# Attention scores from float16 pairs of q and k, one 128-row product a block, exponentials of 1536 columns

## The chip, the core and the metric

The kernel runs on one core of one Trainium2 chip. A core has five engines that run beside each other and wait for one another by semaphores: PE (matrix products into PSUM, eight banks of 512 float32 columns for each of 128 partitions), ACT (functions of one operand), DVE and POOL (arithmetic on tiles), and SP, which here only issues DMAs. The metric is the time of one execution on the device, in microseconds (us); lower is better.

## The reference, cut to what matters

Four layers follow each other on two images of 128 channels and 64 x 64 pixels. The change lies in the first, an attention over all 4096 pixels with four heads of 32 channels:

```python
xn = group_norm(x)                                  # 32 groups
q, k, v = split(w_qkv @ xn + b_qkv)                 # 128 channels each
q, k = rotary(q), rotary(k)                         # by row and column of the pixel
scale = 1 / sqrt(sqrt(32))
weight = einsum('bct,bcs->bts', q * scale, k * scale)       # per head, 4096 x 4096
weight = softmax(weight.astype(float16), axis=-1).astype(float32)
a = einsum('bts,bcs->bct', weight, v)
return xn + w_proj @ a + b_proj
```

The three others (a convolution layer with sampled positions, a 3x3 convolution layer, a state-space layer) are as before.

## The kernel before, in words

**Preparation** (`layer0`, to L253). The images are loaded and normalised into `xa`. For each of 16 blocks of 512 pixels (`rotated`, L177) PE makes two products each for q and k, DVE adds the bias and multiplies by the tables of cosines and sines (L184, L186), POOL adds the two (L188), SP stores the block to DRAM (`qd`, `kd`, L189), and DVE takes the largest magnitude a block later (L190). `values` (L193) makes v: two copies and a cast on ACT (L203, L205, L207), subtractions on POOL (L206, L208); v is kept as three bfloat16 parts and a column block of ones. After block 10 (`n == NBLK + 2`, L223) `load_head` brings the first head back from DRAM. From the largest magnitudes comes a flag (L235 to L250): where the product of the bounds on the norms of q and k is under 81 in each head, the exponentials need no subtraction of a maximum, and `attend` runs; else `attend_any`. This part's order on each engine is as written (`tc.manual_schedule`). The trace shows that `attend` ran.

**Attention** (`attend`, L268). For one head, q (32 channels x 4096 pixels, float32) is held four times, on partitions 0, 32, 64 and 96 of a tile `q4`; k lies in `k4`, each fourth block of 128 keys on another 32 partitions. The work is a list of 2048 units: image, head, block of 512 queries (`qb`, eight), block of 128 keys (`kb`, 32).

- `scores` (L283): one float32 product of 32 rows for each unit into a bank of `ps`; four units in a row lie on the four groups of 32 rows of the array. A group is two units (`GR = 2`), `ps` is a ring of three pairs of banks, and one ACTIVATE (L293) takes the exponential of 1024 columns into a float16 tile `e16` (eight of them).
- `weigh` (L298): for each unit one product of 128 rows, v (bfloat16, weights) by `e16`, added up in a bank `acc` (two) over the 32 key blocks (L303). Row 96 and on of `acc` are the sums of the exponentials.
- `normalise` (L309), after the 32nd: DVE takes the reciprocal (L314), copies it twice, multiplies the three parts (L320); POOL adds them into `att` (L321, L322).
- `project` (L326), for one query block after its last head: a float32 product of `att` by the projection's weights, into a tile of the ring `ps` (L329), added to `xa` by DVE (L331).

The loop (L337) issues four units' scores, then the weighted sums of four older ones; a projection is issued at `kb` 28 of the next query block. The loads of the next head (`load_head`, L259: four DMAs of q and four of k) are issued on SP in the current head. `k4` and `q4` have two tiles each, taken in turn. Outside the preparation the order on each engine comes from the Tile framework's scheduler, and rings of tiles give the waits.

Everything after L256 (the layers 1 to 3) starts when attention has ended.

Of the kernel before, what the change touches and what calls it, by code (L numbers as in the profile page):

```python
# [10 lines left out]
F32 = mybir.dt.float32  # L11
F16 = mybir.dt.float16
# [4 lines left out]
ALU = mybir.AluOpType  # L17
# [44 lines left out]
def img(t):  # L62
    return t.rearrange("p (r w) -> p r w", w=HW)
# [36 lines left out]
def layer0(g, I):  # L100
# [6 lines left out]
    with ExitStack() as ctx:  # L107
# [12 lines left out]
        k4 = [w.tile([P, L // BLK, P], F32, name=f"k4{i}") for i in range(2)]  # L120
# [5 lines left out]
        with ExitStack() as pctx:  # L126
# [119 lines left out]
            ok = pw.tile([1, NB, NH], F32, name="ok")  # L246
            nc.vector.tensor_scalar(ok, pr, 81.0, None, ALU.is_lt)
            okm = pw.tile([1, 1], F32, name="okm")
            nc.vector.tensor_reduce(okm, ok, AX.XY, ALU.min)
            nc.vector.tensor_copy(flag, okm)  # L250

        small = nc.values_load(flag[0:1, 0:1], min_val=0, max_val=1)
        with tc.If(small > 0) as cond:  # L253
            attend(g, v3, wpt, bo, qd, kd, q4, k4)
        with cond.Else():
            attend_any(g, v3, wp3, bo, qd, kd, q4)  # L256


def load_head(g, qd, kd, q4, k4, n):  # L259
    b, h = divmod(n, NH)  # L260
    rows = slice(h * CH, (h + 1) * CH)
    src = kd[b][rows, :].rearrange("p (j r m) -> p j r m", r=4, m=P)
    for r in range(4):
        g.nc.sync.dma_start(k4[n % 2][r * CH : (r + 1) * CH], src[:, :, r, :])
        g.nc.sync.dma_start(q4[n % 2][r * CH : (r + 1) * CH, :], qd[b][rows, :])


def attend(g, v3, wpt, bo, qd, kd, q4, k4):  # L268


    nc, tc = g.nc, g.tc
    NS = L // P
    GR = 2
    with ExitStack() as ctx:
        ap = ctx.enter_context(tc.tile_pool(name="l0ap", bufs=1))
        sm = ctx.enter_context(tc.tile_pool(name="l0asm", bufs=2))
        ep = ctx.enter_context(tc.tile_pool(name="l0ep", bufs=8))
        pss = ctx.enter_context(tc.tile_pool(name="l0pss", bufs=3, space=PSUM))
        psa = ctx.enter_context(tc.tile_pool(name="l0psa", bufs=2, space=PSUM))

        att = {}

        def scores(group):  # L283
            ps = pss.tile([P, GR, BLK], F32, name="ps")
            for i, (b, h, qb, kb) in enumerate(group):
                rows = slice((kb % 4) * CH, (kb % 4 + 1) * CH)
                nc.tensor.matmul(  # L287
                    ps[:, i, :], k4[h % 2][rows, kb // 4, :], q4[h % 2][rows, qb * BLK : (qb + 1) * BLK],
                    start=True, stop=True,
                )  # L290
            e = ep.tile([P, GR, BLK], F16, name="e16")
            n = len(group)
            nc.scalar.activation(e[:, :n, :], ps[:, :n, :], AF.Exp)  # L293
            return e

        acc = None

        def weigh(group, e):  # L298
            nonlocal acc
            for i, (b, h, qb, kb) in enumerate(group):  # L300
                if kb == 0:
                    acc = psa.tile([P, BLK], F32, name="acc")
                nc.tensor.matmul(acc, v3[b][:, kb, h, :], e[:, i, :], start=(kb == 0), stop=(kb == NS - 1))  # L303
                if kb == NS - 1:
                    normalise(b, h, qb, acc)
                    if h == NH - 1:
                        done.append((b, qb))

        def normalise(b, h, qb, acc):  # L309

            if qb == h == 0:
                att[b] = ap.tile([P, L], F32, name="att")
            rec = sm.tile([96, BLK], F32, name="rec")
            nc.vector.reciprocal(rec[0:32], acc[96:128])  # L314
            nc.vector.tensor_copy(rec[32:64], rec[0:32])
            nc.vector.tensor_copy(rec[64:96], rec[0:32])
            parts = sm.tile([CH, 3, BLK], F32, name="parts")
            for j in range(3):
                rows = slice(32 * j, 32 * j + 32)
                nc.vector.tensor_tensor(parts[:, j, :], acc[rows], rec[rows], ALU.mult)  # L320
            nc.gpsimd.tensor_add(parts[:, 0, :], parts[:, 0, :], parts[:, 1, :])  # L321
            nc.gpsimd.tensor_add(  # L322
                att[b][h * CH : (h + 1) * CH, qb * BLK : (qb + 1) * BLK], parts[:, 0, :], parts[:, 2, :]
            )

        def project(b, qb):  # L326

            pp = pss.tile([P, GR, BLK], F32, name="ps")
            nc.tensor.matmul(pp[:, 0, :], wpt, att[b][:, qb * BLK : (qb + 1) * BLK], start=True, stop=True)  # L329
            xv = interior(g, b, qb * RB, RB)  # L330
            nc.vector.scalar_tensor_tensor(xv, img(pp[:, 0, :]), bo, xv, ALU.add, ALU.add)  # L331
# [4 lines left out]
        held, done = [], []  # L336
        for u in range(0, len(units), 4):  # L337

            if done and u % NS == 4 * 7:
                project(*done.pop(0))  # L340

            for i in range(u, u + 4, GR):
                held.append((units[i : i + GR], scores(units[i : i + GR])))
            if len(held) > 8 // GR:
                for i in range(u, u + 4, GR):
                    weigh(*held.pop(0))

            b, h, qb, kb = units[u]
            if qb == 0 and kb == 12 and b * NH + h + 1 < NB * NH:
                load_head(g, qd, kd, q4, k4, b * NH + h + 1)  # L350
        for x in held:
            weigh(*x)
        for x in done:
            project(*x)


def attend_any(g, v3, wp3, bo, qd, kd, q4):
# [3 lines left out]
    with ExitStack() as ctx:  # L361
# [9 lines left out]
        for b in range(NB):  # L371
# [4 lines left out]
            def scores(qt, h):  # L376

                rows = slice(h * CH, (h + 1) * CH)
                s16 = at.tile([P, L], F16, name="s16")
                mx = sm.tile([P, 4], F32, name="mx")  # L380
                for j in range(4):
                    ps = pss.tile([P, 2, BLK], F32, name="ps")
                    for i in range(2):
                        k0 = (2 * j + i) * BLK
                        nc.tensor.matmul(
                            ps[:, i, :],
                            qr[rows, qt * P : (qt + 1) * P],
                            kr[rows, k0 : k0 + BLK],
                            start=True,
                            stop=True,  # L390
                        )
                    nc.vector.tensor_scalar(
                        s16[:, j * 2 * BLK : (j + 1) * 2 * BLK],
                        ps.rearrange("p a b -> p (a b)"),
                        1.0, None, ALU.mult, ALU.max, accum_out=mx[:, j : j + 1],
                    )
# [1432 lines left out]
def _constants():  # L1829
# [8 lines left out]
    scale = 1.0 / np.sqrt(np.sqrt(CH))  # L1838
# [98 lines left out]
```

## Time and profile before

| what | value |
|---|---|
| runs | 5787.97, 5789.0 (median), 5793.07 us |
| span of the profiled execution, first to last instruction | 5785.8 us |
| that execution's time with what lies around the span | not given apart; the median of the runs is 3.2 us above the span |
| granted PE clock over the span | 0.890 |
| preparation, to the first exponential | 121.1 us |
| attention, first exponential to the end of the last | 121.1 to 1247.5 us |
| last projection, to the first load of layer 1 | 1247.5 to 1259.9 us |
| layers 1 to 3 | 1259.9 to 5785.8 us |
| busy over the span: PE, DVE, ACT, POOL | 85%, 76%, 72%, 62% |

How to read it: the page of the profile gives busy times for the span, the same in 40 slices (about 145 us each; attention fills slices 2 to 8), the chain of work that ended last, and groups of instructions by line with the number of instructions, busy time, mean of one, and the idle time ahead of them with what ended it. An arrow `ps<-q,k` is the written tile and what is read. A float32 product stands in the trace as two matmuls, each with its own weight load; the trace gives a matmul's start, and its end is modelled, so that products in a row overlap. PEld is the loading of weights, PEclk the clock granted to PE, as a share of full speed.

### The profile page before, as it was taken

To read this page: it belongs to the slowest core of one execution; us is meant where nothing else is said; L and a number is where in the kernel's file an instruction comes from. 1 tells how busy PE (TensorE), PEld (TensorE's weight loads), DVE (VectorE), ACT (ScalarE), POOL (GpSimd) and SP (SyncE) were. 2 spreads that over 40 slices of the span, in tenths; PEclk is the share of its full clock that TensorE was granted. 3 is DMA by queue.
4 is the path that set the end of the run, shared out by engine and by line. 5 is a ranking of instruction groups with operands and counts; after the bars stand their busy time and mean duration, and the time that the engine had idled before them with its cause. 6 is when DMAs were issued, how large, how long until landed. Compare 5 with 4: busy or idle time off the path is not lost.

```text
span 5785.8 us, 58630 instructions
## 1 busy us (share of the span) xinstructions
PE 4889.5 (85%) x19110; PEld 1740.4 (30%) x19110; DVE 4400.7 (76%) x4135; ACT 4153.4 (72%) x6617; POOL 3602.9 (62%) x1139
## 2 busy tenths in 40 slices
PE   7999999989978789977877778777888877888776
PEld 3333333334434334422222222222222222222221
DVE  5333333355214599779999999999999999999998
ACT  4888888850025621289888888888888888888886
POOL 5111111110010031179999999999999999999998
PEclk8999999999989999988888888888877888877887
DMA  5000001030047400065555655556555555555564
GB/s 158 19 19 19 19 19 33 1 60 1 1 83 124 79 18 0 6 144 128 135 131 132 143 140 130 129 132 149 141 131 134 133 136 143 136 130 135 134 142 102
DMA packets 333114, 541.95 MB, mean 94 GB/s; under 512 B 66384, under 2 KB 121184, under 8 KB 331712
## 3 DMA queue, kind: packets, MB, share of 16 engines
q1 hardware_dynamic: 329664, 534.58, 39.7%
q10 hardware_dynamic: 3136, 3.56, 0.3%
q8 instruction: 151, 2.47, 0.2%
q14 instruction: 163, 1.34, 0.1%
HBM read 448.81 MB, written 89.13 MB: 93 GB/s over the span
## 4 chain that ended last, share of the span: by engine, by line
DVE 42%; PE 38%; ACT 10%; issue 5%; DMA 2%; POOL 2%; SPq 1%; DVEq 0%; POOLq 0%; ACTq 0%
DVE db L1524 28%; PE ps L287 11%; DVE db L1488 10%; PE acc L303 9%; PE m L1078 5%; PE m L566 5%; ACT da L1510 3%; PE acd L812 2%; ACT db L1516 1%; DVE gt L1551 1%; PE m L526 1%; ACT L1375 1%; ACT u L1375 1%; PE pf L775 1%; POOL db L1534 1%
## 5 line engine op out<-in xcount | busy, mean ns | idle before, releaser
L1534 POOL TENSOR_TENSOR db<-db,c 128x2048 f32<-128x2048 f32 x512 | 2313.2, 4533 | 45.4 <-ACT hl L1529 31.4
L1510 ACT ACTIVATE da<-dd,am 128x512 f32<-128x512 f32 x2048 | 1398.4, 687 | 299.1 <-DVE db L1524 280.1
L1524 DVE TENSOR_TENSOR_SCAN db<-da,db 128x512 f32<-128x512 f32 x1376 | 1585.0, 1203 | 34.6 <-ACT db L1516 26.6
L293 ACT ACTIVATE e<-ps 128x1024 f16<-128x1024 f32 x1024 | 992.2, 1021 | 134.2 <-PE ps L287 116.3
L1524 DVE TENSOR_TENSOR_SCAN db<-da,hl,db 128x512 f32<-128x512 f32 x672 | 825.9, 1271 | 40.3 <-POOL db L1497 3.0
L1488 DVE TENSOR_TENSOR db<-pbc,dd 128x2048 f32<-128x2048 f32 (+1 forms) x384 | 781.0, 2034 | 31.7 <-DMA dd<-dx 31.7
L1497 POOL TENSOR_TENSOR db<-b,dd 128x2048 f32<-128x2048 f32 (+1 forms) x192 | 773.2, 4027 | 13.0 <-DMA b<-bx 13.0
L1542 PE MATMUL py<-db,fold 128*32 128x512 f32 x4096 | 600.7, 672 | 151.8 <-POOL db L1534 151.8
L314 DVE RECIPROCAL rec<-acc 32x512 f32<-32x512 f32 x64 | 214.9, 3358 | 638.8 <-PE acc L303 612.1
L321 POOL TENSOR_TENSOR parts<-parts 32x512 f32<-32x512 f32 x64 | 80.4, 1256 | 974.8 <-DVE parts L320 974.8
L287 PE MATMUL ps<-q,k 32*128 32x512 f32 x4096 | 656.0, 642 | 3.6 <-DVE flag L250 2.8
L303 PE MATMUL acc<-e,v 128*128 128x512 f16 x2048 | 531.6, 382 | 0.0
L1516 ACT ACTIVATE db<-da,db,hl 128x1 f32<-128x1 f32 x1120 | 393.7, 352 | 147.3 <-DVE db L1488 103.8
L1078 PE MATMUL m<-v,u 128*128 128x512 f32 x864 | 380.0, 603 | 42.6 <-DVE v L1021 41.6
L1435 PE MATMUL pm<-dd,ident 128*128 128x512 f32 x512 | 357.5, 836 | 2.9 <-ACT dd L1428 2.7
L1467 PE MATMUL pbc<-bc,sel 64*128 64x512 f32 x384 | 208.7, 544 | 123.6 <-DVE db L1488 122.8
L303 PEld LDWEIGHTS <-v 128*128 128x128 bf16 x2048 | 158.3, 97 | 509.4 <-issue 388.0
L1394 PE MATMUL pm<-u,wxp 128*72 128x512 f32 x256 | 182.7, 855 | 141.4 <-ACT u L1375 141.4
L287 PEld LDWEIGHTS ps<-q,k 32*128 32x128 f32 x4096 | 229.7, 184 | 228.1 <-issue 145.2
L566 PE MATMUL m<-comb,w 64*128 64x512 f32 (+4 forms) x1296 | 269.9, 575 | 0.0
L686 POOL TENSOR_SCALAR yt<-y 32x512 f32<-32x512 f32 x8 | 18.2, 2271 | 381.3 <-DVE y L677 380.9
L1542 PEld LDWEIGHTS py<-db,fold 128*32 128x32 f32 x4096 | 89.8, 113 | 542.6 <-issue 313.0
(318 smaller groups left out, 6340.1 us busy)
## 6 DMA issues: line engine op xcount, KB each, us to landing
dd<-dx SPq DMA_DIRECT2D x1024, 256.0 KB, 6.5
dx<-dd SPq DMA_DIRECT2D x128, 512.0 KB, 5.5
c<-bx SPq DMA_DIRECT2D x1024, 64.0 KB, 2.1
hats<-pos SPq DMA_DIRECT2D x136, 256.0 KB, 9.7
b<-bx SPq DMA_DIRECT2D x512, 64.0 KB, 4.7
q<-qd SPq DMA_DIRECT2D x32, 512.0 KB, 7.4
w<-in_conv0T SPq DMA_DIRECT2D x18, 288.0 KB, 8.4
q<-in_x SPq DMA_DIRECT2D x8, 512.0 KB, 7.5
```

The costliest lines, as they stand in the source:

```text
L287: nc.tensor.matmul(ps[:, i, :], k4[h % 2][rows, kb // 4, :], q4[h % 2][rows, qb * BLK : (qb + 1) * BLK], start=True, stop=True,)
L293: nc.scalar.activation(e[:, :n, :], ps[:, :n, :], AF.Exp)
L303: nc.tensor.matmul(acc, v3[b][:, kb, h, :], e[:, i, :], start=(kb == 0), stop=(kb == NS - 1))
L566: yield lambda q=q, dy=dy, src=src, i0=i0, i1=i1: nc.tensor.matmul(m[:, i0 * NF : i1 * NF], w[half, dy, q, x, :], src, start=(dy == KC and ...
L1078: nc.tensor.matmul(m[x], weights[j][:, dy, x, :], v[j][b][:, x, r0 : r0 + RP, :].rearrange("p r i -> p (r i)"), start=(dy == 0), stop=(dy ...
L1488: nc.vector.tensor_tensor(db_tile(k)[:, :, :n], G[k].pop("pb")[:, :n].unsqueeze(1).to_broadcast([P, 4, n]), S[i]["d4", hf][:, 1, :, :n], A ...
L1497: nc.gpsimd.tensor_tensor(db_tile(k)[:, :, n:], S[i]["b", ng][:, n:].unsqueeze(1).to_broadcast([P, 4, BLK - n]), S[i]["d4", hf][:, 1, :, n ...
L1510: nc.scalar.activation(da, S[i]["d4", hf][:, 0, q, :], AF.Exp, scale=am[:, hf, q, ng : ng + 1])
L1516: nc.scalar.activation(b0, da[:, first : first + 1], AF.Identity, bias=b0, scale=hl[:, hf, ng, q, :])
L1524: nc.vector.tensor_tensor_scan(d1, d0, d1, 0.0 if zero else hl[:, hf, ng, q, :], ALU.mult, ALU.add)
L1534: nc.gpsimd.tensor_mul(v, v, S[i]["c", ng].unsqueeze(1).to_broadcast([P, 4, BLK]))
L1542: nc.tensor.matmul(S[i]["y", hf][32 * q : 32 * q + 32, :], fold, G[k]["db"][:, q, :], start=False, stop=(ng == NNG - 1),)
```

## The change

`k4` goes. Each of the two `q4` tiles (16 KB a partition) is seen as a float16 tile `qk` of two halves: q at `[:, 0]`, k at `[:, 1]`, both for 4096 pixels. q and k are scaled up by `UP = 64` in the tables of cosines and sines; the scores are scaled down by 64 squared in the exponential. A value t becomes a pair: its rounding to float16 and the remainder t - rounded, also in float16. Over the four groups of 32 partitions q holds rounded, remainder, rounded, remainder and k holds rounded, rounded, remainder, remainder, so that one product of 128 rows adds all four cross terms.

The rounding is a copy of 128 x 1024 (`split`: ACT for the first head, POOL later), the remainder a subtraction on DVE (64 partitions for k, twice 32 for q). The float32 data comes in pieces of 1024 columns on all four groups (`fetch`: four DMAs), through two staging tiles; the first head's k comes whole into the second `q4` tile. During a head the pieces of the next are fetched at `kb` 4 of query blocks 1 to 4 and split at `kb` 26; in query block 0 of the first head, that head's last two pieces of q. A group is now three units, `ps` two triples of banks, `e16` five tiles; a group's weighted sums are issued after the scores of the second group behind it (`LAG = 2`). The projection takes an `acc` bank and is issued at `kb` 24 to 26 of the next query block. The flag also asks that the bounds of q and of k stay under 376 each. The loop of `attend` is now in the order written.

```diff
-                        load_head(g, qd, kd, q4, k4, 0)
+                        for r in range(4):
+                            nc.sync.dma_start(q4[1][r * CH : (r + 1) * CH, :], kd[0][0:CH, :])
+                        first = [fetch(g, stg, qd, 0, c) for c in range(2)]
+                    elif NBLK + 4 <= n < NBLK + 6:
+                        for c in range(2 * (n - NBLK - 4), 2 * (n - NBLK - 4) + 2):
+                            split(g, qk[0], 1, c, q4[1][:, c * PIECE : (c + 1) * PIECE], nc.scalar.copy)
+                    elif n == NBLK + 6:
+                        for c in range(2):
+                            split(g, qk[0], 0, c, first[c], nc.scalar.copy)
...
+            nc.vector.tensor_scalar(ok[:, 0], pr, 81.0 * UP**4, None, ALU.is_lt)
+            nc.vector.tensor_scalar(ok[:, 1:], hn.rearrange("p b j h -> p j b h"), (376.0 * UP) ** 2, None, ALU.is_lt)
...
+def fetch(g, stg, src, n, c):
+    b, h = divmod(n, NH)
+    t = stg.tile([P, PIECE], F32, name="piece")
     for r in range(4):
+        g.nc.sync.dma_start(
+            t[r * CH : (r + 1) * CH], src[b][h * CH : (h + 1) * CH, c * PIECE : (c + 1) * PIECE]
+        )
+    return t
+
+def split(g, qk, j, c, t, copy):
+    dst = qk[:, j, c * PIECE : (c + 1) * PIECE]
+    copy(dst, t)
+    for p0, p1 in ((64, 128),) if j else ((32, 64), (96, 128)):
+        g.nc.vector.tensor_sub(dst[p0:p1], t[p0:p1], dst[p0:p1])
...
-    GR = 2
+    GR = 3
+    LAG = 2
...
-                rows = slice((kb % 4) * CH, (kb % 4 + 1) * CH)
+                t = qk[h % 2]
                 nc.tensor.matmul(
-                    ps[:, i, :], k4[h % 2][rows, kb // 4, :], q4[h % 2][rows, qb * BLK : (qb + 1) * BLK],
+                    ps[:, i, :], t[:, 1, kb * P : (kb + 1) * P], t[:, 0, qb * BLK : (qb + 1) * BLK],
...
-            nc.scalar.activation(e[:, :n, :], ps[:, :n, :], AF.Exp)
+            nc.scalar.activation(e[:, :n, :], ps[:, :n, :], AF.Exp, scale=1.0 / UP**2)
...
-            pp = pss.tile([P, GR, BLK], F32, name="ps")
-            nc.tensor.matmul(pp[:, 0, :], wpt, att[b][:, qb * BLK : (qb + 1) * BLK], start=True, stop=True)
+            pp = psa.tile([P, BLK], F32, name="acc")
+            nc.tensor.matmul(pp, wpt, att[b][:, qb * BLK : (qb + 1) * BLK], start=True, stop=True)
...
+        with tc.manual_schedule():
+            for u in range(0, len(units), GR):
+                group = units[u : u + GR]
+                b, h, qb, kb = group[0]
+                held.append((group, scores(group)))
+                if done and 24 <= kb < 24 + GR:
+                    project(*done.pop(0))
+                if len(held) > LAG:
+                    weigh(*held.pop(0))
+                if 4 <= kb < 4 + GR:
+                    coming = [(n, j, c, fetch(g, stg, (qd, kd)[j], n, c)) for n, j, c in pieces(b * NH + h, qb)]
+                elif 26 <= kb < 26 + GR:
+                    for n, j, c, t in coming:
+                        split(g, qk[n % 2], j, c, t, nc.gpsimd.tensor_copy)
```

In the changed kernel the scores are L312, the exponentials L318, the weighted sums L328, POOL's last addition L347, the projection L354, and the copy and subtraction of a split L287 and L289.

More of the change, by code (lines that the diff above doesn't have):

```diff
@@ L119, in layer0 @@
         q4 = [w.tile([P, L], F32, name=f"q4{i}") for i in range(2)]
-        k4 = [w.tile([P, L // BLK, P], F32, name=f"k4{i}") for i in range(2)]
+        qk = [t.bitcast(F16).rearrange("p (j l) -> p j l", j=2) for t in q4]
+        stg = ctx.enter_context(tc.tile_pool(name="l0stg", bufs=2))
         qd = [dr.tile([P, L], F32, name=f"qd{b}") for b in range(NB)]
@@ L245, in layer0 @@
             nc.vector.tensor_mul(pr, hn[:, :, 0, :], hn[:, :, 1, :])
-            ok = pw.tile([1, NB, NH], F32, name="ok")
-            nc.vector.tensor_scalar(ok, pr, 81.0, None, ALU.is_lt)
+            ok = pw.tile([1, 3, NB, NH], F32, name="ok")
+            nc.vector.tensor_scalar(ok[:, 0], pr, 81.0 * UP**4, None, ALU.is_lt)
+            nc.vector.tensor_scalar(ok[:, 1:], hn.rearrange("p b j h -> p j b h"), (376.0 * UP) ** 2, None, ALU.is_lt)
             okm = pw.tile([1, 1], F32, name="okm")
-            nc.vector.tensor_reduce(okm, ok, AX.XY, ALU.min)
+            nc.vector.tensor_reduce(okm, ok.rearrange("p i b h -> p (i b h)"), AX.X, ALU.min)
             nc.vector.tensor_copy(flag, okm)
@@ L253, in layer0, with attend @@
         with tc.If(small > 0) as cond:
-            attend(g, v3, wpt, bo, qd, kd, q4, k4)
+            attend(g, v3, wpt, bo, qd, kd, qk, stg)
         with cond.Else():
             attend_any(g, v3, wp3, bo, qd, kd, q4)
-def load_head(g, qd, kd, q4, k4, n):
+PIECE = L // 4
+UP = 64.0
+def fetch(g, stg, src, n, c):
     b, h = divmod(n, NH)
-    rows = slice(h * CH, (h + 1) * CH)
-    src = kd[b][rows, :].rearrange("p (j r m) -> p j r m", r=4, m=P)
+    t = stg.tile([P, PIECE], F32, name="piece")
     for r in range(4):
-        g.nc.sync.dma_start(k4[n % 2][r * CH : (r + 1) * CH], src[:, :, r, :])
-        g.nc.sync.dma_start(q4[n % 2][r * CH : (r + 1) * CH, :], qd[b][rows, :])
-def attend(g, v3, wpt, bo, qd, kd, q4, k4):
+        g.nc.sync.dma_start(
[7 more added lines that the diff above has]
+        g.nc.vector.tensor_sub(dst[p0:p1], t[p0:p1], dst[p0:p1])
+def attend(g, v3, wpt, bo, qd, kd, qk, stg):
     nc, tc = g.nc, g.tc
     NS = L // P
-    GR = 2
+    GR = 3
+    LAG = 2
     with ExitStack() as ctx:
@@ L276, in attend @@
         sm = ctx.enter_context(tc.tile_pool(name="l0asm", bufs=2))
-        ep = ctx.enter_context(tc.tile_pool(name="l0ep", bufs=8))
-        pss = ctx.enter_context(tc.tile_pool(name="l0pss", bufs=3, space=PSUM))
+        ep = ctx.enter_context(tc.tile_pool(name="l0ep", bufs=5))
+        pss = ctx.enter_context(tc.tile_pool(name="l0pss", bufs=2, space=PSUM))
         psa = ctx.enter_context(tc.tile_pool(name="l0psa", bufs=2, space=PSUM))
@@ L326, in project, with pieces @@
         def project(b, qb):
-            pp = pss.tile([P, GR, BLK], F32, name="ps")
-            nc.tensor.matmul(pp[:, 0, :], wpt, att[b][:, qb * BLK : (qb + 1) * BLK], start=True, stop=True)
+            pp = psa.tile([P, BLK], F32, name="acc")
+            nc.tensor.matmul(pp, wpt, att[b][:, qb * BLK : (qb + 1) * BLK], start=True, stop=True)
             xv = interior(g, b, qb * RB, RB)
-            nc.vector.scalar_tensor_tensor(xv, img(pp[:, 0, :]), bo, xv, ALU.add, ALU.add)
+            nc.vector.scalar_tensor_tensor(xv, img(pp), bo, xv, ALU.add, ALU.add)
+        def pieces(n, qb):
+            if n == 0 and qb == 0:
+                return [(0, 0, 2), (0, 0, 3)]
+            if n + 1 < NB * NH and 1 <= qb <= 4:
+                return [(n + 1, 1, qb - 1), (n + 1, 0, qb - 1)]
+            return []
         units = [
@@ L335, in attend @@
         ]
[L336 to L345, printed above, removed]
-                    weigh(*held.pop(0))
[L348 to L354, printed above, removed]
+        held, done, coming = [], [], []
+        with tc.manual_schedule():
[6 more added lines that the diff above has]
+                if len(held) > LAG:
+                    weigh(*held.pop(0))
+                if 4 <= kb < 4 + GR:
[3 more added lines that the diff above has]
+                        split(g, qk[n % 2], j, c, t, nc.gpsimd.tensor_copy)
+                    coming = []
+            for x in held:
+                weigh(*x)
+            for x in done:
+                project(*x)
 def attend_any(g, v3, wp3, bo, qd, kd, q4):
@@ L394, in scores @@
                         ps.rearrange("p a b -> p (a b)"),
-                        1.0, None, ALU.mult, ALU.max, accum_out=mx[:, j : j + 1],
+                        1.0 / UP**2, None, ALU.mult, ALU.max, accum_out=mx[:, j : j + 1],
                     )
@@ L1836, in _constants @@
     freqs = np.concatenate([fh, fw], axis=-1).reshape(L, dh)
-    scale = 1.0 / np.sqrt(np.sqrt(CH))
+    scale = UP / np.sqrt(np.sqrt(CH))
     sign = np.tile(np.array([-1.0, 1.0], np.float32), P // 2)[:, None]
```

## The prediction

> **What bounds the kernel now.** I first split the span into its stages with the table of busy time by stretch, then asked the chain of waits inside the stage that the change touches, then read the groups of instructions of that stage, and last its timeline.
>
> ```profile
> core 0: us, PE busy (x) PEld busy (x) DVE busy (x) ACT busy (x) POOL busy (x), PEclk, DMA share, GB/s
> 121.00:1247.00 1126.00, 1125.19 (x6158) 391.43 (x6157) 404.39 (x393) 991.82 (x1025) 158.36 (x126) 1.00 0.09 18
> 1260.00:5785.00 4525.00, 3676.06 (x12532) 1305.73 (x12532) 3911.11 (x3595) 3117.76 (x5525) 3358.27 (x935) 0.86 0.48 111
> ```
> ```profile
> by line: PE ps L287 54.7%; PE acc L303 44.0%; PE ps L329 1.1%; ACT L293 0.1%; ACT e L293 0.1%; issue 0.0%
> ```
>
> Attention lasts from the first exponential at 121.1 to the end of the last at 1247.5: 1126.4 us. There PE has no idle time at a granted clock of 1.00, ACT is busy 88%, and the chain is PE alone: scores (L287) and weighted sums (L303). The 4525 us after it are not touched.
>
> ```profile
> L293 ACT ACTIVATE e<-ps 128x1024 f16<-128x1024 f32 x1024 | 992.2, 1021 | 134.2 <-PE ps L287 116.3
> L287 PE MATMUL ps<-q,k 32*128 32x512 f32 x4096 | 656.0, 642 | 3.6 <-DVE flag L250 2.8 <-ACT e L293 0.8
> L303 PE MATMUL acc<-e,v 128*128 128x512 f16 x2048 | 531.6, 382 | 0.0
> L303 PEld LDWEIGHTS <-v 128*128 128x128 bf16 x2048 | 158.3, 97 | 509.4 <-issue 388.0
> ```
> ```profile
> 700.79 1.94 ACT L293 ACTIVATE e<-ps 128x1024 f16<-128x1024 f32 x2 [0.96 <-PE ps L287]
> 700.95 1.04 PE L303 MATMUL acc<-e,v 128*128 128x512 f16 x4
> 703.95 1.40 PE L287 MATMUL ps<-q,k 32*128 32x512 f32 x8
> 705.28 0.55 PEld L303 LDWEIGHTS <-v 128*128 128x128 bf16 x4 [0.76 <-issue]
> 705.28 1.04 PE L303 MATMUL acc<-e,v 128*128 128x512 f16 x4
> 706.25 1.14 PE L287 MATMUL ps<-q,k 32*128 32x512 f32 x8
> ```
>
> The trace has 2048 score blocks (eight query blocks, 32 key blocks, four heads, two images); a float32 product stands as two matmuls. Four blocks take two exponentials, eight L287 and four L303. Read two steps from the timeline. Four L303 span 1.04, one lasts 0.38, so they start (1.04-0.38)/3 = 0.22 us apart, each with its own weight load of 0.097, which is therefore covered. From 703.95 to 705.28 four blocks of scores take 1.33 us, 0.33 a block. Two exponentials span 1.94 and one lasts 1.02, so ACT back to back needs 1.94-1.02 = 0.92 for two blocks. PE's four blocks come to 0.97+1.33 = 2.30 there (705.28 to 706.25, and 703.95 to 705.28), ACT's to 1.84: PE is late, ACT is next. Per block the stage runs at 1126.4/2048 = 0.55 us.
>
> **The change, part by part.** *Scores.* Each block becomes one float16 matmul of 128 rows and 512 columns. The nearest row is L303: same rows, columns and two-byte operands, 0.22 us, weight load hidden. A group is now three blocks: three scores, three weighted sums, 6 x 0.22 = 1.32 us of PE.
>
> *Exponentials.* 1536 columns cost the 0.92 step plus 512 columns. Two slopes bound those: ACT's evictions of pf (L789) take 587 ns for 512 columns and 220 for 64, 0.82 ns a column; L203 (583 ns, 512 columns) against L293 (1021, 1024) gives 0.86. So 0.42 to 0.44, and a step of 1.34 to 1.36. I take 1.36, because each hand-over also passes a wait. There are 682 full groups and one of two: 682 x 1.36 + 0.94 = 928 us. PE's 1.32 lies beside it with 0.04 to spare: **ACT becomes the bound**, but hardly. The score ring falls from three pairs of banks to two triples; a triple is ready 3 x 0.22 + 0.16 of drain (0.38-0.22) + about 0.2 for both hand-overs = 1.0 after ACT frees it, inside 1.36.
>
> The Trainium skill (ScalarE: Activation LUTs, What ACT_TABLE_LOAD costs) gives 186 ns plus 0.833 a column for an ACTIVATE without pointer operands, with 93 ns overlapped: 0.946 at 1024 columns and 1.373 at 1536. The trace has 0.92 for the first; by the rule the stage would be 938, 10 us longer.
>
> *Projections* (L329) move from the score ring to the acc ring. The next acc takes the same bank and waits for the addition that empties it, some 10 us old by then: nothing. Each holds PE 0.95 us (1243.38 to the next score at 1244.33). That was in the old time; now ACT has 0.34 of cover (1.36-1.0), so 15 x 0.6 = 9 us; the sixteenth stands after the end, as before.
>
> *A wait that gets tight.* A projection needs att, and PE queues every later product behind it.
>
> ```profile
> 706.36 3.36 DVE L314 RECIPROCAL rec<-acc 32x512 f32<-32x512 f32 x1 [5.94 <-PE acc L303]
> 710.65 2.11 DVE L320 TENSOR_TENSOR parts<-acc,rec 32x512 f32<-32x512 f32 x3
> 713.46 1.25 POOL L322 TENSOR_TENSOR att<-parts 32x512 f32<-32x512 f32 x1
> ```
>
> From rec to the end of att is 714.71-706.36 = 8.35, with hand-overs about 8.6. The projection stands seven groups after the last weighted sum, less that group's rest: 6 x 1.36 + 0.66 + 0 to 0.44 = 8.8 to 9.3. It fits by 0.2 if DVE is free.
>
> *Splits inside attention.* Per head eight POOL copies of 128x1024 and twelve DVE subtractions, in four query blocks. A subtraction: L506, two float32 operands from SBUF, takes 1.36 for 1152 columns, so 1.2. A POOL copy is not in the trace: MEMSET (3.51 for 4096 columns) gives 0.9, POOL's additions (1.26 for 512) 2.5, L686 (2.27 for 512) 4.5. I take 2, between a write alone and a two-input operation. DVE has 1126-404 = 722 us idle and POOL 968, so the work is hidden, except that rec queues behind the subtractions. These wait for the copies, which start when POOL is done with att, and end 2 x 2 + 2 x 1.2 = 6.4 later; rec is wanted some 5.5 after that point. Late by 0.9, it hits only the four projections of image 0 whose query blocks also split: 4 x 0.9, 4 us. At 0.9 nothing, at 4.5 4 x 5.7 = 23. A copy waits for its load, and behind it on POOL stand only the additions of the same query block; behind a load on SP that waits for a staging buffer stands only the next load.
>
> *Loads.* 4 MB a head in 32 issues on SP, against 2.5 MB in 8; the DMA share is 0.09 and SP has nothing else there. A pair of pieces has some 20 blocks (9 us) to land: hidden.
>
> *Before attention.* The first head is split by ACT and DVE while the projection of q and k runs. There DVE stands behind ACT, ACT behind POOL:
>
> ```profile
> 93.68 0.75 DVE L184 SCALAR_TENSOR_TENSOR rt<-pq,vecs,cs 128x512 f32<-128x512 f32 x1 [0.76 <-PE pq L182]
> 95.44 0.62 ACT L207 CAST v<-v 128x512 bf16<-128x512 f32 x1 [2.44 <-POOL v L206]
> 102.53 1.27 POOL L188 TENSOR_TENSOR rt<-rt,rt 128x512 f32<-128x512 f32 x1 [4.77 <-DMA qd<-rt]
> ```
>
> In block 12 two copies (0.62 + 0.43 = 1.05 each) follow the cast that ends at 96.06, and two subtractions follow them: DVE reaches the next L184 at 96.06+2.1+1.2 = 99.4 instead of 93.7, +5.7. Block 13 becomes a closed round: two rotations 2.8, reduction 0.7, POOL 1.3+1.2, cast 0.6, copies 2.1, subtraction 1.2 = 9.9 against the present 4.67, +5.2. Block 14 has four subtractions of q behind its first copy, 1.05+4.8 in place of 2.1+1.2, +7.8. Sum 18.7, less the 4.8 that POOL waits today for a store behind the loads, which now falls into this time: 13.9. The second test of the guard adds 1.0 (L247 takes 1.01), the shorter first scores take off about 0.8. I take +14; all work in idle time would give +4 (eight subtractions, 9.6, less DVE's idle 6.1 between 97.7 and 103.8), no overlap with the present wait +20.
>
> **Sum**, against the profiled execution: 5785.8 - 1126.4 + 928 + 9 + 4 + 14 = 5614.4. The median of the runs is 5789.0, 3.2 above that span, for what lies around it and the spread: **5618 us**, 3.0% faster.
>
> **Rivals.**
> 1. *PE stays the bound.* One weight load per group uncovered, where a waiting score stops the loads behind it: 1.32+0.097 = 1.42, 683 x 1.42 = 970, so 5660. Against it: loads are covered in L303's rows; for it: only 0.04 to spare, and L287's loads show 82.5 us of waiting for ACT.
> 2. *The projection's wait.* POOL copies of 4.5 us: +19, 5637; with all 15 projections 2 us late as well, about 5667. POOL reads beside DVE could do it. In layer 3 POOL's additions (L1534) take 4.53 for 2048 columns, 2.2 ns each, beside DVE scans of two inputs with both engines nine tenths busy, and 2.5 ns in attention with DVE idle: no sign of blocking. The Trainium skill (SBUF — State Buffer, Who interferes with whom) has a DVE instruction with two SBUF inputs and a POOL instruction that reads SBUF lock each other out. By that rule a subtraction would wait out the second copy, 1.1 us at four projections, and one POOL operation of 1.3 for each of the eight before attention: 14 more.
> 3. *A lower clock.* Full rows nearly without pause at 0.81 instead of 1.00, as the later slices show 0.8: 1.32/0.81 = 1.63, 1113 us, so 5803: 0.2% over the median, no change that shows. Against it: 1.00 all through attention.
> 4. *Slower: no weight load is covered.* Scores and sums now change weights of all 128 rows at every product; if each load stood in line, 6 x (0.22+0.097) = 1.90, 1298 us, so 5988. It decides from (1126.4-13-14)/683 = 1.61 a group, 0.05 a product. Against it again L303, four in a row with four loads.
> 5. *The change does not run*: the guard's new limits send it to the general path. The old limit (product of the norms under 81) was met, and 376 for one factor is far off: 1%.
>
> **Chances.** Forecast (5590 to 5640) 0.62, rival 1 0.16, rival 2 0.12, rival 3 0.04, rivals 4 and 5 0.06. The range 5590 to 5690 holds the forecast and rivals 1 and 2: its low end is a step of 1.34 and +4 before attention, its high end rival 1 with +20 there and copies of 4.5. Faster by over 0.2% (what a measurement of this kernel can tell) 0.90, same 0.04, slower 0.06.
>
> **What will show it.** Exponentials of about 1.45 that follow each other every 1.36, ACT over 95% busy and PE with small waits for ACT: the forecast. PE without idle time and ACT waiting for L312 at each group: rival 1. PE waiting for POOL's att (L347) at L354: rival 2. PEclk under 1.00: rival 3. First exponential near 135 instead of 121: the part before attention. I am wrong if the exponential costs more over three banks than its columns say, or if weight loads of two operands that alternate are not covered as those of one are.

## The result, and the profile after

The changed kernel takes 5609.4 us (median of four runs, 5604.5 to 5613.1), against 5791.0 us (5788.0 to 5794.2) for the kernel before on the same chip: a ratio of 0.9686, 95% interval 0.9672 to 0.97. The forecast was 5618 us, with a range of 5590 to 5690.

The profiled execution took 5610.1 us, with a span of 5608.3. Its busy time by stretch (preparation, attention, layers 1 to 3; the columns are those of the prediction's first fence):

```profile
13.00:136.00 123.00, 88.27 (x408) 42.75 (x409) 83.35 (x139) 47.54 (x73) 75.41 (x64) 0.85 0.43 144
136.00:1063.30 927.30, 925.54 (x4119) 401.37 (x4118) 531.63 (x481) 919.33 (x684) 217.10 (x184) 1.00 0.12 35
1076.00:5608.00 4532.00, 3714.52 (x12532) 1313.10 (x12532) 3910.67 (x3595) 3118.36 (x5525) 3358.27 (x935) 0.85 0.48 110
```

Attention now lasts from 136.4 to 1063.3 us, 926.9 in place of 1126.4, at a granted clock of 1.00 as before. ACT is busy 919 of 927 us, 99%. PE is shown busy 926 of 927, but a PE that is drawn busy is not one that sets the pace, as the ends of its products are modelled; who waits for whom must tell. The groups of the page:

```profile
L318 ACT ACTIVATE e<-ps 128x1536 f16<-128x1536 f32 (+1 forms) x683 | 919.0, 1624 | 7.9 <-PE ps L312 7.9
L312 PE MATMUL ps<-q 128*128 128x512 f16 x2048 | 554.0, 379 | 4.3 <-DVE flag L260 2.7
L328 PE MATMUL acc<-e,v 128*128 128x512 f16 x2048 | 553.7, 379 | 0.1
L312 PEld LDWEIGHTS <-q 128*128 128x128 f16 x2048 | 197.7, 97 | 278.5 <-issue 103.6
```

The first row is the answer: ACT waits 7.9 us for PE in the whole stage, where it waited 116 us before. (Its mean of 1624 ns is longer than a step because an exponential's record starts while the one before still runs; one that starts on an idle ACT lasts 1.45 us.) The timeline, in the middle of a query block:

```profile
497.32 11.13 ACT L318 ACTIVATE e<-ps 128x1536 f16<-128x1536 f32 x8
...
500.44 0.81 PE L312 MATMUL ps<-q 128*128 128x512 f16 x3
...
501.08 0.81 PE L328 MATMUL acc<-e,v 128*128 128x512 f16 x3
...
501.78 0.81 PE L312 MATMUL ps<-q 128*128 128x512 f16 x3
```

One group spans 501.78 - 500.44 = 1.34 us. Inside it the sums start 0.64 after the scores, three products of 0.215, and the next scores 0.70 after the sums: 0.645 of products and some 0.05 of waiting for ACT. The start-to-start step of the 683 exponentials has a median of 1.341 us, a mean of 1.358. As starts run ahead, the cleaner measure is from the end of one exponential to the end of the next: 1.343 us in the median, and between 1.339 and 1.346 in 662 of 682 steps. Seventeen steps are clearly longer: the second and third of the stage, and the fifteen at a projection (L354). One of these:

```profile
502.69 5.76 ACT L318 ACTIVATE e<-ps 128x1536 f16<-128x1536 f32 x4
508.87 1.45 ACT L318 ACTIVATE e<-ps 128x1536 f16<-128x1536 f32 x1 [0.42 <-PE ps L312]
```

Where the time went, stage by stage: attention -199.5, preparation +15.2 (first exponential 121.1 to 136.4), everything behind the last exponential +6.7; sum -177.5 of span. The instructions of that last part are the same. It took 4545.0 us here and 4538.3 before, and between 4536.3 and 4546.4 in the eleven experiments below, so the 6.7 lies within what it varies by; what makes it vary is not shown.

### The profile page after: what moved, and what is told of

It is laid out like the page before. It is cut to its first block, busy times and chain, and to the rows that moved or that the text cites. A ratio compares the mean times of both kernels' runs of the same rounds, so it can differ in the third digit from the quotient of the medians.

```text
span 5608.3 us, 54471 instructions
## 1 busy us (share of the span) xinstructions
PE 4731.0 (84%) x17062; PEld 1757.8 (31%) x17062; DVE 4537.0 (81%) x4232; ACT 4086.5 (73%) x6282; POOL 3661.7 (65%) x1197
## 4 chain that ended last, share of the span: by engine, by line
DVE 45%; PE 35%; ACT 11%; issue 5%; DMA 2%; POOL 1%; SPq 1%; DVEq 0%; ACTq 0%; POOLq 0%
DVE db L1558 30%; DVE db L1522 11%; PE ps L312 8%; PE acc L328 8%; PE m L1112 5%; PE m L600 5%; ACT da L1544 4%; PE acd L846 2%; ACT db L1550 1%; DVE gt L1585 1%; PE m L560 1%; ACT L1409 1%; ACT u L1409 1%; PE pf L809 1%; DMA hats<-pos 1%
## 5 line engine op out<-in xcount | busy, mean ns | idle before, releaser
L318 ACT ACTIVATE e<-ps 128x1536 f16<-128x1536 f32 (+1 forms) x683 | 919.0, 1624 | 7.9 <-PE ps L312 7.9
L1576 PE MATMUL py<-db,fold 128*32 128x512 f32 x4096 | 615.6, 687 | 153.2 <-POOL db L1568 153.1
L312 PE MATMUL ps<-q 128*128 128x512 f16 x2048 | 554.0, 379 | 4.3 <-DVE flag L260 2.7
L328 PE MATMUL acc<-e,v 128*128 128x512 f16 x2048 | 553.7, 379 | 0.1
L1428 PE MATMUL pm<-u,wxp 128*72 128x512 f32 x256 | 196.7, 913 | 141.0 <-ACT u L1409 141.0
L312 PEld LDWEIGHTS <-q 128*128 128x128 f16 x2048 | 197.7, 97 | 278.5 <-issue 103.6
L328 PEld LDWEIGHTS <-v 128*128 128x128 bf16 x2048 | 199.3, 97 | 248.8 <-issue 10.2
```

Of the source, the lines that this page charges most:

```text
L312: nc.tensor.matmul(ps[:, i, :], t[:, 1, kb * P : (kb + 1) * P], t[:, 0, qb * BLK : (qb + 1) * BLK], start=True, stop=True,)
L318: nc.scalar.activation(e[:, :n, :], ps[:, :n, :], AF.Exp, scale=1.0 / UP**2)
L1576: nc.tensor.matmul(S[i]["y", hf][32 * q : 32 * q + 32, :], fold, G[k]["db"][:, q, :], start=False, stop=(ng == NNG - 1),)
```

## The experiments

All are edits of the changed kernel, but for the second, which builds on the kernel before. The theory was: ACT sets attention's step since two-byte scores took PE below it; the wider exponential is worth little by itself; the rest is the splits ahead of attention and the projections. The chief rival was that PE still sets it, or that another part of the change brings the gain.

**Exponentials of 1024 columns** (e1).

```diff
-    GR = 3
+    GR = 2
-        ep = ctx.enter_context(tc.tile_pool(name="l0ep", bufs=5))
-        pss = ctx.enter_context(tc.tile_pool(name="l0pss", bufs=2, space=PSUM))
+        ep = ctx.enter_context(tc.tile_pool(name="l0ep", bufs=8))
+        pss = ctx.enter_context(tc.tile_pool(name="l0pss", bufs=3, space=PSUM))
```

> The changed kernel with exponentials of 1024 columns again (groups of two, three pairs of PSUM banks, eight e16 tiles); the float16 pair product stays. My theory (the cheaper products carry the gain; the width only saves ACT's fixed part): ACT needs 0.92 for two blocks, PE 4 x 0.2155 + 0.05 = 0.91, so 1024 x 0.925 = 947 us and some 5 for projections: attention 952 instead of 927, the kernel about 5634, 25 above the changed one. Rival (the wide exponentials carry most of the gain): attention 1075 and more, the kernel about 5760.

Measured: 5626.8 us, ratio 0.9716 (0.97 to 0.9733); attention 944.0, median step 0.916. I had expected 952. The width is worth 944.0 - 926.9 = 17 us of the 200.

**The wide loop with float32 scores** (e2): the kernel before, with the new loop, its groups of three and its projections, but without splits.

```diff
-    GR = 2
+    GR = 3
+    LAG = 2
...
-        pss = ctx.enter_context(tc.tile_pool(name="l0pss", bufs=3, space=PSUM))
+        pss = ctx.enter_context(tc.tile_pool(name="l0pss", bufs=2, space=PSUM))
```

> The kernel before with everything of the new loop (groups of three, exponentials of 1536, two triples of banks, lag of two groups, projection in an acc bank, written order), but with the float32 products of 32 rows and the old loads. My theory: PE sets the step, and three instead of four products side by side make it worse: 0.31 + 0.53 + 0.52 for the scores and 2 x 0.22 for the rest of the weighted sums, 1.8 a group, 683 x 1.8 = 1229 us of attention, the kernel about 5890, slower than before. Rival (order and width carry the gain): attention under 1000, about 5650.

Measured: 5918.2 us (one run), attention 1256.8, step 1.818. Busy time of its attention, columns as above:

```profile
121.00:1378.00 1257.00, 1255.64 (x6160) 358.33 (x6159) 404.42 (x393) 990.13 (x684) 158.29 (x126) 1.00 0.08 17
```

ACT falls to 79%: PE sets the step again. Groups of three cut the runs of four scores that share the array's four groups of rows: in the traces three float32 scores take 1.07 us to the next weighted sum, where four took 1.22 in the median (1.07 to 1.34) in the kernel before. That costs more than the width gives (attention 28 us above what I expected, 130 above the kernel before). So the width is worth something only with the two-byte scores, while these alone, in the new loop (e1), bring 1126.4 - 944.0 = 182 of the 200 us. The new order of the loop was not run by itself.

**Scores over 32 rows, float16** (e3).

```diff
+                rows = slice((kb % 4) * CH, (kb % 4 + 1) * CH)
-                    ps[:, i, :], t[:, 1, kb * P : (kb + 1) * P], t[:, 0, qb * BLK : (qb + 1) * BLK],
+                    ps[:, i, :], t[rows, 1, kb * P : (kb + 1) * P], t[rows, 0, qb * BLK : (qb + 1) * BLK],
```

> The changed kernel, but each score is a float16 product of 32 rows, on the group of rows that kb picks, so that three lie side by side; it computes one of the four cross terms of the score. My theory (the two-byte type makes the product cheap, not the 128 rows): a score group is 0.31 + 0.31 and PE needs about 1.06 a group, ACT stays the bound at 1.335, projections cost less: attention about 915, the kernel 5597. Rival (the product must fill 128 rows, because changing between 32 and 128 rows drains PE at each group): 0.22 x 6 plus two changes of 0.1 to 0.3, 1.5 to 1.9 a group, 5720 or more.

Measured: 5602.1 us, 0.9674 (0.9658 to 0.969); attention 918.6. The row of its scores:

```profile
L313 PE MATMUL ps<-q 32*128 32x512 f16 x2042 | 268.7, 381 | 124.0 <-ACT e L319 122.9
```

This kernel leaves out three of the four cross terms. PE now has 124 us of idle time, nearly all of it waiting for ACT, and the stage is only 8 us shorter. The median step between starts is 1.331 in place of 1.341, but from end to end it is 1.343 in both: ACT's pace does not move when PE has room. The 8 us lie in the longer steps alone, which exceed the median by 9.8 us in all in the changed kernel (17 steps) and by 1.3 here (3 steps). So the 128 rows, which carry the three further cross terms, cost 8 us, nearly all at the projections. What makes the scores cheap is the two-byte type: e2 and e3 both have 32 rows in groups of three, and their scores keep PE busy for 774.0 and 268.7 us.

**ACT a third shorter** (e7).

```diff
-            nc.scalar.activation(e[:, :n, :], ps[:, :n, :], AF.Exp, scale=1.0 / UP**2)
+            m = min(n, 2)
+            nc.scalar.activation(e[:, :m, :], ps[:, :m, :], AF.Exp, scale=1.0 / UP**2)
...
-                nc.tensor.matmul(acc, v3[b][:, kb, h, :], e[:, i, :], start=(kb == 0), stop=(kb == NS - 1))
+                nc.tensor.matmul(acc, v3[b][:, kb, h, :], e[:, min(i, 1), :], start=(kb == 0), stop=(kb == NS - 1))
```

> The changed kernel with exponentials of 1024 of the 1536 columns: one block's exponential in three is left out, and its weighted sum uses its neighbour's. All products stay, so this shows PE's own limit. My theory (ACT sets the step at 1.345 and PE is only a little behind): 683 x 1.30 and 15 projections in full, 13, so attention about 901, the kernel 5583. Rival (PE has ample room and only ACT counts): 683 x 0.93 = 635, 5317. Rival (PE already sets the step): no change, 5609.

Measured: 5583.2 us (one run); attention 900.1, median step 1.295 = 6 x 0.216. ACT's wait in this kernel between 140 and 1035 us (total us, times, longest):

```profile
ACT e L319 <- PE ps L312: 199.4, 668, 1.5
```

ACT waits for PE at nearly every group, where it did so 17 times in the changed kernel. The bound has changed sides, and the two limits lie 1.343 - 1.295 = 0.048 us apart, 3.6%.

**A third of the weighted sums left out** (e8), the counterpart.

```diff
+                if kb % 3 != 1 or kb == NS - 1:
-                nc.tensor.matmul(acc, v3[b][:, kb, h, :], e[:, i, :], start=(kb == 0), stop=(kb == NS - 1))
+                    nc.tensor.matmul(acc, v3[b][:, kb, h, :], e[:, i, :], start=(kb == 0), stop=(kb == NS - 1))
```

> One weighted sum in three is left out (those of kb = 1, 4, 7, ...), so that TensorE has five products a group in place of six; the exponentials are unchanged. It leaves part of the sums out, and serves to show ScalarE's own limit. Theory (ScalarE sets the step, TensorE is 3% behind it): the exponentials follow each other every 1.33 to 1.34 us, none is late at a projection, attention 908 to 917 us, the kernel 5590 to 5600 us. Rival (TensorE still sets most steps): the step falls by 0.1 us or more, towards 5 x 0.216 = 1.08, attention below 860 and the kernel below 5545 us.

Measured: 5606.2 us (one run); attention 923.3, median step 1.341, unchanged.

```profile
ACT e L318 <- PE ps L312: 4.1, 16, 0.7
```

ACT sets the step: 0.216 us less PE work a group moves it by nothing. But the expectation missed: the projections are still late, 1.76 us in place of 1.98 at most of them, so 4 us were saved and not 10 to 19. The long step fell by 0.215, just the one product left out between two triples; the slack of the groups ahead was of no use, which fits the ring: with two triples of `ps` PE can't work further ahead than one group. A deeper ring was not tried.

**The projection in two halves** (e4), in successive groups.

```diff
-                    project(*done.pop(0))
+                    project(*done[0], 0)
+                elif done and 24 + GR <= kb < 24 + 2 * GR:
+                    project(*done.pop(0), 1)
```

> The changed kernel with each projection as two products of 256 columns, the second one group later. PE's work is the same. My theory (a projection of 0.86 us goes beyond ACT's cover of about 0.3 and stops ACT for 0.64, 15 times; halves of 0.43 fit): 9 us less, attention 918, the kernel 5600. Rival (PE sets the step, so work moved on PE changes nothing): 5609.

Measured: 5607.7 us, 0.969 (0.9677 to 0.9704); attention 927.5, against 926.9. My theory of a saving fell: the steps over 1.8 us between starts went from 16 to 2, but 21 of 1.70 to 1.73 stand in their place, and the mean step stayed (1.3585 against 1.3576). A group has only 0.048 us to catch up in, so that two halves in a row are late together by about what one whole is. A gain of up to 2 us would not show: attention varies by 3 us between kernels that are alike in it (925.7 to 928.5).

**Less splitting ahead of attention** (e5): the second half of k and the second quarter of q are split when attention has begun.

```diff
-                    elif NBLK + 4 <= n < NBLK + 6:
-                        for c in range(2 * (n - NBLK - 4), 2 * (n - NBLK - 4) + 2):
-                            split(g, qk[0], 1, c, q4[1][:, c * PIECE : (c + 1) * PIECE], nc.scalar.copy)
+                    elif n == NBLK + 4:
+                        for c in range(2):
+                            round16(g, qk[0], 1, c, q4[1][:, c * PIECE : (c + 1) * PIECE], nc.scalar.copy)
...
+            for c in range(2, 4):
+                split(g, qk[0], 1, c, k32[:, c * PIECE : (c + 1) * PIECE], nc.gpsimd.tensor_copy)
+            split(g, qk[0], 0, 1, first[1], nc.gpsimd.tensor_copy)
```

> The changed kernel with less splitting ahead of attention: there only two pieces of k and one of q, and each subtraction stands one block after its rounding, so that DVE does not stand behind ACT and POOL; the last two pieces of k and the second of q are split at the start of attention by POOL and DVE. My theory (the 15 us came from DVE waiting in line): first exponential at about 126 instead of 136.4, the kernel about 5599; the late pieces of k are needed at key blocks 16 and 24, 7 and 11 us after the start, and are done by 4 and 5. Rival (DVE's added work counts, not its place in line): 4 of 8 subtractions less, 5 us, 5604. Rival (what is saved returns as PE waiting for k): 5609.

Measured: 5666.4 us, 0.9794 (0.978 to 0.9807). The first exponential came at 124.6, 11.8 earlier, as meant; attention took 1003.6, 77 longer. Part of its timeline, cut to SP's loads, POOL and DVE:

```profile
188.53 1.22 DVE L302 TENSOR_TENSOR q<-piece,q 64x1024 f16<-64x1024 f32 x1 [2.97 <-POOL q L295]
189.78 1.70 SPq L281 DMA_DIRECT2D piece<-qd  x4
194.08 1.04 POOL L295 CAST q<-piece 128x1024 f16<-128x1024 f32 x1 [5.58 <-DMA piece<-qd]
195.15 2.47 DVE L302 TENSOR_TENSOR q<-piece,q 32x1024 f16<-32x1024 f32 x2 [5.40 <-POOL q L295]
197.65 3.36 DVE L352 RECIPROCAL rec<-acc 32x512 f32<-32x512 f32 x1
```

q's loads are issued only when k's subtraction has ended (189.75): all quarters went through one staging tile. I take it that the tile of `first[1]`, used inside the branch, held the other for good; e10 and e9 test it. The reciprocal of the finished query block stands behind this on DVE, and after it `acc`, the weighted sums and the exponentials. The whole and the halves together (**e6**, e5 and e4 in one kernel) gave the same picture: 5674.1 us, 0.9802 (0.9788 to 0.9815), first exponential 123.4, attention 1008.6.

> The two edits together: half projections and less splitting ahead. My theory: the two savings add up, 9 and 10, the kernel about 5590. Rival: what the one saves the other had covered, 5600.

**One staging tile, and nothing else** (e10).

```diff
+        one = ctx.enter_context(tc.tile_pool(name="l0one", bufs=1))
-                    coming = [(n, j, c, fetch(g, stg, (qd, kd)[j], n, c)) for n, j, c in pieces(b * NH + h, qb)]
+                    coming = [(n, j, c, fetch(g, one, (qd, kd)[j], n, c)) for n, j, c in pieces(b * NH + h, qb)]
```

> The changed kernel, with the splitting ahead as it is, but the quarters fetched during attention all go through one staging tile in place of two. Theory (one tile makes q's load wait for k's split, and the splits, DVE's reciprocals and with them the weighted sums and the exponentials come late): first exponential stays at 136, attention 985 to 1005 us in place of 927, the kernel 5668 to 5688 us. Rival (one tile does no harm, since 30 us lie between two pairs of quarters): attention 927, kernel 5609.

Measured: 5682.2 us (one run); first exponential 137.6, attention 1001.6. The waits of this kernel between 140 and 1060 us:

```profile
DVE q L289 <- POOL q L287: 227.4, 53, 5.4
POOL q L287 <- DMA piece<-qd: 172.4, 30, 7.3
...
ACT e L319 <- PE ps L313: 76.5, 38, 6.7
...
PE acc L329 <- DVE parts L346: 41.0, 16, 4.4
```

Read them as a chain: POOL waits for the late load, DVE for POOL, PE for the `acc` that DVE empties late, ACT for PE. In the changed kernel the first two rows are 79.7 and 1.1, and the last is not there. Over the whole of attention ACT waits 79.3 us for PE here and 7.9 in the changed kernel, which is nearly all that attention loses (1001.6 - 926.9 = 74.7); in e5 it waits 81.1, where 76.7 were lost. One staging tile alone thus makes e5's loss; e9 is the counterpart.

**Less splitting ahead, two staging tiles** (e9): e5, with q's second quarter fetched inside attention.

```diff
-                        first = [fetch(g, stg, qd, 0, c) for c in range(2)]
+                        first = fetch(g, stg, qd, 0, 0)
...
+            split(g, qk[0], 0, 1, fetch(g, stg, qd, 0, 1), nc.gpsimd.tensor_copy)
```

> As in the earlier run with less splitting ahead, k's first half and q's first quarter alone are split before attention; but q's second quarter is fetched and split inside attention, so that no staging tile of the preparation is held across the branch, and k's and q's quarters come to alternate between two staging tiles again, as in the changed kernel. Theory (the earlier loss of 77 us was the one shared staging tile, not the splits at the start of attention): first exponential at 125 to 126 us (changed kernel 136.4), attention 927 us as in the changed kernel, the kernel about 11 us below 5609, 5597 to 5601 us. Rival (it was the four splits at the start of attention, or less cover of some other kind): attention stays at about 1000 us and the kernel at 5666.

Measured: 5591.0 us (5588.4 to 5602.2), ratio 0.9664 (0.9651 to 0.9678): the best full kernel of the study. The first exponential came at 122.9 and attention took 925.7, so the 77 us of e5 were the staging tile's. By the medians it is 18 us below the changed kernel, by the ratios 13, as the kernel before was 3 us faster beside it too. The two profiled spans differ by 21.8: 13.5 ahead of attention, 1.2 in it, and 7.0 in the layers behind, which vary by that much between runs. The two intervals still touch between 0.9672 and 0.9678, so the times alone do not separate the two kernels; the first exponential does (122.9 against 136.4 to 139.5 in the eight kernels that split ahead as the changed one). Which half of the edit brings it, fewer splits or subtractions one block later, was not separated.

**Rounding on DVE** (e11).

```diff
-                        split(g, qk[n % 2], j, c, t, nc.gpsimd.tensor_copy)
+                        split(g, qk[n % 2], j, c, t, nc.vector.tensor_copy)
```

> The rounding copies of attention's splits (58 of 128x1024, 1.04 us each on POOL) are made by DVE in place of POOL. Theory (a subtraction of two SBUF tiles takes 2.03 us in place of 1.22 us because a POOL copy runs at that moment): all 88 subtractions of attention take 1.21 to 1.24 us, 107 us in sum in place of 127. Rival (they are long for another reason, the loads or where they stand): some two dozen of them stay at 2.03. In both, DVE stays below 70% of attention and the kernel's time at 5605 to 5613 us, since DVE isn't what a group waits for; if the splits come late by this, a few projections wait for less or more of their cover, 2 us either way.

Measured: 5603.8 us (one run); attention 928.5. Two dozen subtractions stayed long, as my rival had it, but not for its reason:

```profile
175.52 1.15 DVE L287 CAST q<-piece 128x1024 f16<-128x1024 f32 x1
...
176.19 1.59 POOL L347 TENSOR_TENSOR att<-parts 32x512 f32<-32x512 f32 x1
...
176.70 2.17 DVE L289 TENSOR_TENSOR q<-piece,q 64x1024 f16<-64x1024 f32 x1
```

They now meet POOL's addition to `att` instead of its copy. In both kernels the length is the rest of the POOL instruction plus 1.08 us: 0.95 + 1.08 = 2.03 in 24 of the changed kernel's, 1.08 + 1.08 = 2.17 in all 24 here. Where POOL is idle a subtraction takes 1.22. The theory's cause stands, POOL at work; its number fell, as I had thought of POOL's copies alone and not of its additions.

## Why the prediction was right, point by point

- *The bound.* ACT becomes it, "but hardly": e7 and e8 show this from both sides, 1.343 for ACT and 1.295 for PE, and e3 keeps ACT's 1.343 with PE idle for 13% of the stage. Rival 1 (one weight load a group uncovered) did not happen, nor rival 4: six products take 1.295 us with a fresh weight load each, so none is exposed. Rival 3 (lower clock) is excluded by the 1.00 above.
- *The exponential's step.* I took 1.36 of 1.34 to 1.36; 1.343 from end to end was measured. The extra 0.02, taken because each hand-over also passes a wait, is not there; 682 x 0.017 = 12 us, most of attention's difference (941 foreseen, 926.9 measured). The rest is the next point, less 1 us for the two long steps at the start. The page of the Trainium skill that I weighed (ScalarE: Activation LUTs, What ACT_TABLE_LOAD costs) gave 1.373; the trace has 1.343, 2% less.
- *Projections.* 15 x 0.6 = 9 us foreseen for the product and 4 for late splits. From end to end the fifteen long steps have 8.5 us over the median in all: 0.53 for an ordinary one (1.87), and 0.68 for four (2.02) at which PE also waits some 0.15 for `att`. These four are not the ones of my mechanism, a reciprocal that stands behind the splits of image 0. They are two in each image, though the last head of image 1 splits nothing, and in the last head of image 0 every reciprocal starts 0.04 us after the last weighted sum, behind splits too. They are the query blocks, every third, whose projection is issued at `kb` 24 and not 25 or 26, closest behind its sums; there I had found the chain to fit by 0.2, and it misses by some 0.15. So the splits delayed nothing here: a POOL copy took 1.04 us, at the low end of my bounds of 0.9 to 4.5, where I had said "nothing", and not 2.
- *Splits ahead of attention.* First exponential foreseen near 135, found at 136.4. The profile shows the closed rounds on DVE:

```profile
98.68 2.36 DVE L289 TENSOR_TENSOR q<-q,q 64x1024 f16<-64x1024 f32 x2 [6.45 <-ACT q L287]
...
108.91 2.36 DVE L289 TENSOR_TENSOR q<-q,q 64x1024 f16<-64x1024 f32 x2 [3.93 <-ACT q L287]
...
119.14 4.96 DVE L289 TENSOR_TENSOR q<-piece,q 32x1024 f16<-32x1024 f32 x4 [3.92 <-ACT q L287]
```

  The rounds from one to the next are 10.2 us (9.9 foreseen for block 13) and 10.2 us, then 5.0 of four subtractions (4.8 foreseen). The first subtractions end 1.7 us later than in my working (101.07 against 99.4), as ACT's first copies wait for a load that I had left out:

```profile
97.60 1.99 ACT L287 CAST q<-q 128x1024 f16<-128x1024 f32 x2 [2.24 <-DMA q<-kd]
```

  One reading of the working was wrong without weight: between 97.7 and 103.8 DVE was idle for 4.8 us, not 6.1, as L184 and L186 run in between, so that all work in idle time would have given +5 and not +4.
- *What I judged wrongly, without harm.* Against the rule of the Trainium skill (SBUF — State Buffer, Who interferes with whom) I read from layer 3's rows "no sign of blocking". The subtractions show blocking: one that starts beside a POOL instruction waits out its rest (e11). It costs 24 x 0.81 = 19 us of DVE in attention, and the reciprocals ahead of the projections did not come late by it. The eight subtractions ahead of attention met no POOL instruction and took 1.22 each, so the wait that rival 2 added for them did not come; the 14 that it gives for both is 4.4 + 10.4 = 14.8. Why DVE's scans and POOL's additions of layer 3 run side by side is open; it wasn't tried.
- *The sum.* Against a span of 5614.4 came 5608.3: attention -14, preparation +1, the part behind attention +7. That last lies within what this part varies by, so a good share of the closeness is luck: without it the span would have been 13 below the forecast and not 6.

## What to carry to other kernels

When a change moves the bound to the next engine, ask at once how far the old one is behind: here 3.6%, so that neither a shorter ACT (26 us of 927) nor a shorter PE (4 to 8 us) is worth much alone, and the next gain lay outside the stage, in what delayed its start. Splitting ahead only what the first key blocks need brought the first exponential forward by 13.5 us. A ring's depth is worth checking after every edit of who holds a tile: a staging tile too few cost 77 us where the edit was to gain 10.

## What the runs showed of the hardware

- Products of 128 rows and 512 columns with two-byte operands follow each other every 0.215 to 0.216 us though each brings its own weight load of 0.097, also where the weights alternate between float16 and bfloat16.
- ACT's exponentials end every 0.917 us with 1024 columns (the kernel before, e1) and every 1.343 with 1536 (nine kernels here), also where PE is idle for 124 us (e3).
- 32-row scores in float16 (e3) keep PE busy for 268.7 / 2042 = 0.13 us each in groups of three, half of the 554.0 / 2048 = 0.27 of 128-row ones by the same measure.
- DVE and POOL: see e11; a subtraction of two SBUF tiles takes 1.22 us alone, and the rest of POOL's instruction plus 1.08 us beside it. POOL was held up too: its addition, which starts beside DVE's rounding copy there, took 1.59 us in place of 1.26.
